# SAGE's neighbour sums over three bf16 pieces of h, and the second attention's scores on VectorE, in a four-layer graph network

## The chip, the cores and the metric

The kernel runs on one core of one Trainium2 chip. The metric is the device time of one execution in microseconds, taken as the median of several runs. The engines are named as in the profile: PE is TensorE (PEld its weight loads), DVE is VectorE, ACT is ScalarE, POOL is GpSimd, and SP issues most of the DMA transfers. L12 is line 12 of the kernel before.

## The reference

The input is x, 3327 nodes of 512 float32 features, and adj, a sparse adjacency matrix. Four layers follow each other, each of the form x = x + layer(relu(layernorm(x)), adj). Layer 0 is a graph attention with 8 heads of 64, followed by a batch normalisation and a relu; layer 1 is SAGE; layers 2 and 3 are graph attentions with an elu. What matters here are SAGE and the scores of layer 2:

```python
# layer 1, x is here h = relu(layernorm(x))
mask = (adj > 0).astype(x.dtype)
deg = jnp.sum(mask, axis=1, keepdims=True)
agg = mask @ x / jnp.maximum(deg, 1.0)
self_f = x @ W_self + b_self
nb_f = agg @ W_nb + b_nb
combined = jnp.concatenate([self_f, nb_f], axis=-1)
out = combined @ W_comb + b_comb
return jax.nn.relu(out)
# layer 2
Wh = jnp.einsum('nd,hdo->hno', x, W)
f1 = jnp.einsum('hno,ho->hn', Wh, a1)
f2 = jnp.einsum('hno,ho->hn', Wh, a2)
e = jax.nn.leaky_relu(f1[:, :, None] + f2[:, None, :], negative_slope=ALPHA)
e = jnp.where(adj[None, :, :] > 0, e, NEG_INF)
attention = jax.nn.softmax(e, axis=-1)
h_prime = jnp.einsum('hnm,hmo->hno', attention, Wh)
```

## The kernel before

Nodes are padded to 3328 and cut into 26 blocks of 128 rows. At the start the kernel builds, from adj, lists of neighbours: each block is two groups of 64 destination rows (GB), and each group has a number of chunks of 128 source rows (CAPS, from 22 for the first group down to 4 for the last; 359 chunks in all). A chunk is fetched by one indirect DMA on GpSimd (`gather`, L1115), which reads 128 rows of a table in DRAM by the indices in a column of `idx`. `mask` (one byte per element, in SBUF) says which of the 128 sources belong to which of the 64 destinations.

The three attentions (`attend`) walk the chunks in batches of three: VectorE makes the weights (L1216, L1223) and TensorE sums the weighted rows (L1237). Their order on TensorE, VectorE and ScalarE is written by hand.

Between the first and second attention lies the region that the change touches. There the order of the instructions on each engine is settled by the framework's scheduler, from the program's order, dependences and buffers. Its steps are these.

- The batch normalisation's variance (`var_ps`, up to about 945 us in the profile).
- `normed(c)` (L1364 and after), for two blocks at a time: VectorE scales and shifts (L1370, L1371), takes the relu and the residual (L1372), the statistics (L1377, L1378), and ScalarE writes h = Relu(r x + ng) (L1385) into `bn_y`. SP stores h to `h_dram` (L1386), 2048 bytes per row, one store of 512 KB per two blocks.
- `own(c)` (L1388 and after), for each block: four transposes (`h_ps`), ScalarE's copy (`hT`, L1393), four 512-column fp32 matmuls with W_self W_comb (`s_ps`, L1396), and VectorE's addition of the bias (L1397). It stands two blocks behind `normed`.
- SAGE's loop. A part is two chunks of each of the block's two groups. `load` takes a row buffer `z_rows` (128 x 2 x 512 float32) and a mask buffer `z_mask` for each group, of which there are SROWS = 8 each, so 16 chunks; ScalarE widens the mask to float32 (L1453), and GpSimd gathers. Loading runs two parts (SAHEAD) ahead. Then, for each chunk in turn of the two groups u = 0 and 1, TensorE does one float32 matmul (L1472), mask 128x64 as weights, rows 128x512 as data, into half the partitions of `sage_acc`: `acc[u * GB : (u + 1) * GB, :]`.
- Ahead of each pair of chunks stands a `tick()`, which advances all that lies beside the loop by one step. The first of it is `ending` (L1409 and after): the mean (`s_ag`, ScalarE), transposes (`a_ps`), copy (`aT`), four matmuls with W_nb W_comb (`n_ps`, L1421), the sum with `own`'s result and the residual on VectorE (L1426, L1427), and the store of x2. The second is the next layer's projection, the class `Following`: `norm` does the layernorm on ScalarE (L777 to L788), and `rest` the remaining six steps: transposes (`p_ps`, L795) and ScalarE's Relu (L798); the scores `p_sd` as four matmuls of 16 columns with WA, a product of W and the attention vectors made at the start (L803), and two exps (L807, L808) and a copy (L810) of them on ScalarE; a clamp (L813) and four matmuls `p_wh` = hW (L816); eight ScalarE multiplications by the exps, one per head, and the store of the table's rows (L820, L821); a transpose `p_tr` (L824); and its copy and store (L827 and after). The PSUM buffers of `Following` are two, shared by `p_ps`, `p_sd`, `p_wh` and `p_tr`.

`following(...)` makes this class, and its constructor loads W (1 MB, `fWt`) by SP. For layer 2 it is called ahead of the variance; for layer 3 the same class runs beside the second attention.

Of the kernel before, what the change touches and what calls it, by code (L numbers as in the profile page):

```python
# [23 lines left out]
F32 = mybir.dt.float32  # L24
BF16 = mybir.dt.bfloat16

F32R = mybir.dt.float32r
I32 = mybir.dt.int32
# [3 lines left out]
AF = mybir.ActivationFunctionType  # L32
ALU = mybir.AluOpType
ET = mybir.EngineType
AX = mybir.AxisListType
# [3 lines left out]
P = 128  # L39
H = 8  # L40
F = 64
D = H * F
# [15 lines left out]
UNIT = 3  # L58
SUNIT = 2
SROWS = 8  # L60
SAHEAD = 2
SMALL = 53.0
SHIFT = 20.0
# [676 lines left out]
class Following:  # L740

    def __init__(self, tc, cs, N, wl, W, WA, table, r_dram, pool, psum, pb=1):
        self.__dict__.update(locals())
        nc = tc.nc
        self.NB = table.shape[0] // P
        self.Wt = pool.tile([P, KC, D], F32, name=f"fWt{wl}")
        nc.sync.dma_start(self.Wt, W.rearrange("(kc p) o -> p kc o", p=P))
        self.hs = pool.tile([P, self.NB, KC], F32, name=f"hs{wl}")  # L750
        self.early, self.ready = [], []
# [4 lines left out]
    def tick(self):  # L756
        for _ in range(min(2, len(self.ready))):
            while self.ready and next(self.ready[0]) is None:
                self.ready.pop(0)
        for g in list(self.early):  # L760
            hx = next(g)
            if hx is not None:
                self.early.remove(g)
                self.ready.append(self.rest(*hx))

    def drain(self):
        while self.early or self.ready:
# [4 lines left out]
    def norm(self, c, xt):  # L772
        nc, pp, cs = self.tc.nc, self.pool, self.cs

        junk = pp.tile([P, D], F32, name="ln_j", tag="ln_j", bufs=1)
        st = pp.tile([P, 4], F32, name="ln_s", tag="ln_s", bufs=3)
        nc.scalar.activation(junk, xt, AF.Identity, accum_out=st[:, 0:1])  # L777
        nc.scalar.mul(st[:, 1:2], st[:, 0:1], -1.0 / D)
        nc.scalar.activation(junk, xt, AF.Square, bias=st[:, 1:2], accum_out=st[:, 2:3])
        step = rsqrt(nc, pp, cs, st[:, 2:3], 1.0 / D)  # L780
        yield
        y = step()
        if c == self.NB - 1:
# [5 lines left out]
        yield c, hx  # L789

    def rest(self, c, hx):
        nc, pp, WA, wl = self.tc.nc, self.pool, self.WA, self.wl
# [294 lines left out]
def sparse(ctx: ExitStack, tc: tile.TileContext, t: dict, out: bass.AP, WA, ls, cs, idx, rdeg, first):  # L1087
# [158 lines left out]
            while ends:  # L1246
                later()

    def following(lx, layer, wl, W, pb=1):
# [5 lines left out]
        return Following(tc, cs, N, wl, W, WA, table, r_dram, pp, pps, pb)  # L1255

    def elu_into(xin, dst, then=lambda c, xt: None):
        def finish(c, hp, pool):
# [17 lines left out]


    wx_dram = dram.tile([2, KC, P, D], F32, name="wx_dram")
    h_dram = dram.tile([NP, D], F32, name="h_dram")
    with ExitStack() as mx:  # L1280
        mid = mx.enter_context(tc.tile_pool(name="fmid", bufs=1))

# [58 lines left out]
        Wx = mid.tile([P, 2, KC, D], F32, name="fWx")  # L1341
        nc.sync.dma_start(Wx, wx_dram.rearrange("k kc p o -> p k kc o"))

        proj = following(mx, 2, 1, t["L2_gnn_W"], 2)
        gp = mx.enter_context(tc.tile_pool(name="fsage", bufs=2))
        gps = mx.enter_context(tc.tile_pool(name="fsage_ps", bufs=2, space=PSUM))
        two = [P, 2, D]
# [15 lines left out]
        with tc.tile_pool(name="fln", bufs=1) as bp:  # L1363


            def normed(c):
                xr = bp.tile(two, F32, name="bn_x", tag="bn_x", bufs=3)
                nc.sync.dma_start(xr, t["x"][c * P : (c + 2) * P, :].rearrange("(k p) o -> p k o", p=P))
                yy = y[:, c : c + 2, :]
                nc.vector.tensor_tensor(yy, yy, gam.unsqueeze(1).to_broadcast(two), ALU.mult)  # L1370
                nc.vector.tensor_tensor(yy, yy, bet.unsqueeze(1).to_broadcast(two), ALU.add)  # L1371
                nc.vector.scalar_tensor_tensor(xr, yy, 0.0, xr, ALU.max, ALU.add)  # L1372
                nc.sync.dma_start(x1[c * P : (c + 2) * P, :].rearrange("(k p) o -> p k o", p=P), xr)
                mv = bp.tile([P, 2, nc.vector.BN_AGGR_DIM], F32, name="ln_mv", tag="ln_mv", bufs=3)
                for i in range(2):
                    st = bp.tile([P, nc.vector.BN_STATS_DIM], F32, name="ln_st", tag="ln_st", bufs=3)
                    nc.vector.bn_stats(st, xr[:, i, :])  # L1377
                    nc.vector.bn_aggr(mv[:, i, :], st)  # L1378
                r = rsqrt(nc, bp, cs, mv[:, :, 1:2].rearrange("p k o -> p (k o)"))()
                if c + 2 == NB:  # L1380
                    nc.vector.tensor_tensor(r[:, 1:2], r[:, 1:2], cs["real"], ALU.mult)
                ng = bp.tile([P, 2, 1], F32, name="ln_ng", tag="ln_ng", bufs=3)
                nc.vector.scalar_tensor_tensor(ng, mv[:, :, 0:1], -1.0, r.unsqueeze(2), ALU.mult, ALU.mult)
                for i in range(2):
                    nc.scalar.activation(yy[:, i, :], xr[:, i, :], AF.Relu, scale=r[:, i : i + 1], bias=ng[:, i, :])  # L1385
                nc.sync.dma_start(h_dram[c * P : (c + 2) * P, :].rearrange("(k p) o -> p k o", p=P), yy)  # L1386

            def own(c):  # L1388
                tp = gps.tile([P, KC, P], F32, name="h_ps", tag="a_ps")
# [14 lines left out]
            for i in range(2):  # L1404
                own(NB - 2 + i)

        ends = []

        def ending(b, acc):  # L1409
# [34 lines left out]
        def load(i):  # L1444
            if i >= len(parts):
                return
            zs = loaded[i] = []
            for u, kn in enumerate(parts[i][1]):
                if kn is not None:
                    k0, n = kn  # L1450
                    zt = gp.tile([P, SUNIT, D], F32, name="z_rows", tag="z_rows", bufs=SROWS)
                    mf = gp.tile([P, SUNIT, GB], F32, name="z_mask", tag="z_mask", bufs=SROWS)
                    nc.scalar.copy(mf[:, :n, :], mask[:, k0 : k0 + n, :])  # L1453
                    for k in range(n):
                        gather(zt[:, k, :], h_dram, k0 + k)
                        zs.append((k, u, k0 + k, mf[:, k, :], zt[:, k, :]))
            zs.sort(key=lambda x: x[:2])
# [3 lines left out]
        for i, (b, _, begins, stops) in enumerate(parts):  # L1461
            load(i + SAHEAD)
            if begins:
                acc = gps.tile([P, D], F32, name="sage_acc", tag="sage_acc")
            at = -1
            for r, u, k, m, z in loaded.pop(i):
                if r != at:
                    at = r
                    tick()
                g = b * PG + u  # L1470
                f, l = k == ls.first[g], k == ls.first[g] + CAPS[g] - 1
                nc.tensor.matmul(acc[u * GB : (u + 1) * GB, :], m, z, start=f, stop=l)  # L1472
            if stops:
                ends.append(ending(b, acc))
        while ends:
# [97 lines left out]
```

## Time and profile before

| | us |
|---|---|
| median of 3 runs (2575.82 to 2585.8) | 2585.0 |
| profiled execution | 2951.92 |
| its span | 2950.1 |
| mean granted TensorE clock in it | 0.791 |

The profiled execution is 367 us longer than the median; all times of instructions below are from it. Its stages, with the busy time of each engine, are:

| stage | us from the start | PE | DVE | ACT | POOL | clock |
|---|---|---|---|---|---|---|
| lists and first projection | 0 to 330 | 213 | 215 | 134 | 25 | 0.79 |
| first attention | 330 to 900 | 413 | 456 | 177 | 334 | 0.81 |
| variance | 900 to 945 | 30 | 24 | 17 | 0 | 0.81 |
| `normed` and most of `own` | 945 to 1025 | 68 | 74 | 35 | 0 | 0.92 |
| rest of `own`, SAGE's loop, second projection | 1025 to 1650 | 518 | 67 | 249 | 339 | 0.92 |
| second attention, third projection | 1650 to 2300 | 480 | 475 | 311 | 340 | 0.76 |
| third attention | 2300 to 2950 | 441 | 471 | 193 | 343 | 0.66 |

A line of the table of stages in the profile gives a window and its length, then for each engine the busy time and the number of instructions, the clock as a share of full speed, the mean busy share of the 16 DMA engines, and GB/s. A line of the groups gives line, engine, operation, out<-in, shapes and count; after the first bar the busy time and the mean ns of one; after the second the idle time of the engine ahead of these instructions and what ended it. A line of the timeline gives start, duration, instruction, and in brackets the idle time before it and what ended it. A line of the DMA queues gives packets, MB, and the time the packets took as a share of 16 engines' time; q0 carries GpSimd's gathers, q1 the transfers of SP.

### The profile page before, as it was taken

The page shows a single profiled execution, that of the slowest core. Times are in us where ns is not written, and L with a number is a line of the kernel's source. Part 1 is how long each engine was busy: PE and PEld are TensorE (multiplying, and loading weights), DVE is VectorE, ACT ScalarE, POOL GpSimd, SP SyncE. Part 2 cuts the span into 40 slices and gives each one's busy share as a digit, 9 for nine tenths or more (in the row PEclk, how much of TensorE's full clock was granted, in tenths as well). Part 3 has the DMA queues.
Part 4 walks back from the last instruction along what each step waited for, and adds up shares of the span by engine and source line. Part 5 has one row for each costly group of instructions (what it writes and reads, how often), then busy time and mean ns, then how long its engine had stood idle before and what let it go on. Part 6 is the DMA issues. An engine that isn't in the chain of part 4 may idle for free.

```text
span 2950.1 us, 54237 instructions
## 1 busy us (share of the span) xinstructions
PE 2161.4 (73%) x21320; PEld 1372.2 (47%) x21320; DVE 1781.5 (60%) x2194; ACT 1115.7 (38%) x4044; POOL 1381.8 (47%) x1482
## 2 busy tenths in 40 slices
PE   4777577767775976888998567877777657767775
PEld 2444354555552422233333355655555345556564
DVE  7648587878786800011111377777776277888886
ACT  4543022333434412344455213555666501232333
POOL 1001365666550055665554365555444066666563
PEclk9778688977777997899999777777787766675765
DMA  7761577877662746666665466666565166667774
GB/s 309 282 251 46 174 235 233 252 214 209 201 203 82 246 145 187 189 207 212 198 196 183 133 184 186 200 198 188 178 178 166 45 192 190 193 200 198 201 205 131
DMA packets 188773, 562.09 MB, mean 191 GB/s; under 512 B 37732, under 2 KB 42272, under 8 KB 185182
## 3 DMA queue, kind: packets, MB, share of 16 engines
q0 software_dynamic: 115456, 404.86, 47.2%
q1 hardware_dynamic: 73054, 153.67, 14.7%
q8 instruction: 171, 2.80, 0.4%
q14 instruction: 92, 0.75, 0.1%
HBM read 498.74 MB, written 59.68 MB: 189 GB/s over the span
## 4 chain that ended last, share of the span: by engine, by line
PE 54%; issue 16%; ACT 9%; another core or an unknown queue 3%; DVE 3%; DMA 2%; POOL 1%; SPq 0%; DVEq 0%; ACTq 0%; POOLq 0%
PE facc L1237 28%; PE p_wh L816 7%; PE sage_acc L1472 5%; PE n_ps L1421 3%; PE r_bc L1148 2%; PE p_sd L803 2%; PE s_ps L1396 2%; ACT v_row L820 2%; ACT fhp L1175 1%; PE fwx_ps L1314 1%; PE bmean_ps L1324 1%; PE p_ps L795 1%; ACT hT L798 1%; DMA rows<-table,idx 1%
## 5 line engine op out<-in xcount | busy, mean ns | idle before, releaser
L1115 POOL DMA_INDIRECT rows<-table,idx x1077 | 1023.4, 950 | 873.2 <-PE facc L1237 361.7
L1237 PE MATMUL facc<-rows,wgt 128*64 128x65 f32 x17232 | 975.3, 268 | 412.7 <-issue 394.5
L1237 PEld LDWEIGHTS facc<-rows,wgt 128*64 128x64 f32 x17232 | 826.5, 176 | 628.7 <-issue 576.9
L1223 DVE TENSOR_TENSOR wgt<-mx,mask 128x1536 f32<-128x1536 f32 (+1 forms) x405 | 638.4, 1576 | 158.6 <-PE facc L1237 75.0
L1216 DVE TENSOR_TENSOR mx<-r_bc,rows 128x1536 f32<-128x1536 f32 (+1 forms) x405 | 639.6, 1579 | 144.7 <-PE facc L1237 65.9
L1115 POOL DMA_INDIRECT z_rows<-h_dram,idx x359 | 339.4, 945 | 387.0 <-ACT hT L1393 139.5
L1175 ACT ACTIVATE fhp<-sums,rd 64x64 f32<-64x64 f32 x832 | 219.8, 334 | 137.0 <-DVE rd L1169 71.8
L1472 PE MATMUL sage_acc<-z_rows,z_mask 128*64 128x512 f32 x718 | 225.2, 639 | 9.5 <-DMA z_rows<-h_dram,idx 6.2
L816 PE MATMUL p_wh<-fWt,hT 128*128 128x512 f32 x416 | 227.7, 695 | 1.4 <-ACT s_col L810 1.4
L1165 ACT COPY sums<-facc 128x260 f32<-128x260 f32 x156 | 57.7, 370 | 405.0 <-PE facc L1237 354.3
L813 DVE TENSOR_SCALAR s_col<-s_col 128x8 f32<-128x8 f32 x52 | 9.2, 177 | 306.0 <-issue 135.9
L1208 ACT ACTIVATE mask<-on 128x192 uint8<-128x192 uint16 (+1 forms) x135 | 46.5, 344 | 378.8 <-DVE on L1202 214.1
L816 PEld LDWEIGHTS p_wh<-fWt,hT 128*128 128x128 f32 x416 | 90.3, 228 | 109.8 <-issue 105.3
L820 ACT ACTIVATE v_row<-p_wh,v_row 128x64 f32<-128x64 f32 x416 | 90.4, 328 | 125.8 <-PE p_wh L816 99.3
L1426 DVE TENSOR_TENSOR s_o<-n_ps,bn_y 128x512 f32<-128x512 f32 x26 | 18.0, 691 | 192.2 <-issue 95.6
L1036 POOL DMA_DIRECT2D list_b<-shift x12 | 5.9, 503 | 273.4 <-DVE shift L990 273.4
L680 PE MATMUL wh_ps<-fWt,hT 128*128 128x512 f32 x208 | 128.9, 777 | 0.0
L803 PE MATMUL p_sd<-WA,hT 128*128 128x16 f32 x416 | 74.4, 303 | 70.3 <-ACT hT L798 46.2
L803 PEld LDWEIGHTS p_sd<-WA,hT 128*128 128x128 f32 x416 | 71.8, 246 | 103.9 <-ACT hT L798 59.6
L1175 ACT ACTIVATE bn_y<-sums,rd 64x64 f32<-64x64 f32 x416 | 109.5, 333 | 2.4 <-DVE rd L1169 0.5
L1421 PE MATMUL n_ps<-fWx,aT 128*128 128x512 f32 x208 | 106.1, 646 | 5.6 <-ACT aT L1417 5.5
L1148 PE MATMUL r_bc<-r_two,fones 2*128 2x512 f32 x156 | 95.3, 615 | 14.8 <-issue 8.1
(198 smaller groups left out, 2108.0 us busy)
## 6 DMA issues: line engine op xcount, KB each, us to landing
adj_i<-in_adj SPq DMA_DIRECT2D x26, 1664.0 KB
table<-v_row SPq DMA_DIRECT2D x78, 264.0 KB
rows<-table,idx POOLq DMA_INDIRECT x1077
fin_x<-fx SPq DMA_DIRECT2D x52, 256.0 KB
ln_x<-in_x SPq DMA_DIRECT2D x26, 256.0 KB
bn_x<-in_x SPq DMA_DIRECT2D x13, 512.0 KB
fx<-bn_x SPq DMA_DIRECT2D x13, 512.0 KB
fsage_x<-fx SPq DMA_DIRECT2D x26, 256.0 KB
```

The lines of the kernel that those rows point to most:

```text
L680: nc.tensor.matmul(wh, hT[:, kc, :], self.Wt[:, kc, :], start=(kc == 0), stop=(kc == KC - 1))
L803: nc.tensor.matmul(sd[:, : 2 * H], hT[:, kc, :], WA[wl][:, kc, :], start=(kc == 0), stop=(kc == KC - 1))
L816: nc.tensor.matmul(wh, hT[:, kc, :], self.Wt[:, kc, :], start=(kc == 0), stop=(kc == KC - 1))
L820: nc.scalar.mul(V[:, h, 0:F], wh[:, h * F : (h + 1) * F], V[:, h, F : F + 1])
L1115: nc.gpsimd.indirect_dma_start(out=dst, out_offset=None, in_=src[:, :], in_offset=bass.IndirectOffsetOnAxis(ap=idx[:, k : k + 1], axis=0))
L1148: nc.tensor.matmul(rb, ones[0:2, :].bitcast(F32R), rrs.pop(g).bitcast(F32R), start=True, stop=True)
L1175: nc.scalar.mul(hp[o0 : o0 + GB, h * F : (h + 1) * F], sm[mine, q, 0:F], rd[mine, q, :])
L1216: nc.vector.tensor_tensor(mx[:, :n], rbs[g].unsqueeze(1).to_broadcast(full), gt[:, :n, H * (F + 1) : ROW].unsqueeze(3).to_broadcast(full), ...
L1223: nc.vector.tensor_tensor(wt[:, :n], mx[:, :n], mk.unsqueeze(2).to_broadcast(full), ALU.mult)
L1237: nc.tensor.matmul(accs[g][v * GB : (v + 1) * GB, q * (F + 1) : (q + 1) * (F + 1)], wt[:, k, h, :], gt[:, k, h * (F + 1) : (h + 1) * (F + 1)],
L1421: nc.tensor.matmul(ps, aT[:, kc, :], Wx[:, 1, kc, :], start=(kc == 0), stop=(kc == KC - 1))
L1472: nc.tensor.matmul(acc[u * GB : (u + 1) * GB, :], m, z, start=f, stop=l)
```

## The change

Each row of h is kept in DRAM as three bf16 pieces, high, middle and low, whose sum is h exactly: the upper halves of the float32 words of h, the upper halves of what remains, and the rest. `h_dram` has rows of 3 x 512 bf16, 3072 bytes. In `normed`, per block, VectorE does two subtractions and ScalarE two copies for that, and there is one store of 384 KB per block. The loop gathers these rows, and each chunk is summed by three bf16 matmuls with a bf16 mask into the same accumulator. For a pair of chunks the order is piece by piece, within a piece group by group.

For layer 2, the second part of `Following` is a new function, `rest_by_rows`. It has no `p_sd`: VectorE multiplies `p_wh` with both attention vectors (broadcast to all partitions, 2 x 256 KB loaded in the constructor), sums over each head's 64 columns, and clamps; and it multiplies by the exps in one instruction in place of ScalarE's eight. It has five steps where `rest` has six. Layer 3 still uses `rest`. `following(...)` for layer 2 is now called behind `normed` and `own`, just ahead of the loop; in the built order of SP's instructions its loads come right behind the last store to `h_dram`.

```diff
@@ Following.__init__
+        if ab is not None:
+            self.ab = pool.tile([P, 2, D], F32, name=f"ab{wl}")
+            for k, a in enumerate(ab):
+                nc.sync.dma_start(self.ab[:, k, :], a.partition_broadcast(P))
@@ Following.tick
-                self.ready.append(self.rest(*hx))
+                self.ready.append((self.rest if self.ab is None else self.rest_by_rows)(*hx))
@@
+    def rest_by_rows(self, c, hx):
...
+        yield True
+        self.mean(c, hT)
+        wh = self.psum.tile([P, D], F32, name="p_wh", tag="p_ps", bufs=self.pb)
+        for kc in range(KC):
+            nc.tensor.matmul(wh, hT[:, kc, :], self.Wt[:, kc, :], start=(kc == 0), stop=(kc == KC - 1))
+        yield True
+        pr = pp.tile([P, 2, D], F32, name="sd_pr", tag="sd_pr", bufs=1)
+        nc.vector.tensor_tensor(pr, wh.unsqueeze(1).to_broadcast([P, 2, D]), self.ab, ALU.mult)
+        sd = pp.tile([P, 2 * H], F32, name="sd_col", tag="sd_col", bufs=2)
+        nc.vector.tensor_reduce(sd, pr.rearrange("p k (h f) -> p (k h) f", f=F), AX.X, ALU.add)
+
+        sf = pp.tile([P, H], F32, name="s_col", tag="s_col", bufs=2)
+        nc.vector.tensor_scalar(sf, sd[:, :H], -SMALL, SMALL, ALU.max, ALU.min)
...
+        rs = halves(nc, pp, self.cs, sf)
+        yield True
+        nc.vector.tensor_tensor(
+            V[:, :, 0:F], wh.rearrange("p (h f) -> p h f", f=F), V[:, :, F : F + 1].to_broadcast([P, H, F]), ALU.mult
+        )
+        nc.sync.dma_start(self.table[c * P : (c + 1) * P, :ROW], row.bitcast(I32))
+        rs = rs()
+        yield True
...
@@ sparse
-    h_dram = dram.tile([NP, D], F32, name="h_dram")
+    h_dram = dram.tile([NP, PIECES * D], BF16, name="h_dram")
@@ ahead of the variance
-        proj = following(mx, 2, 1, t["L2_gnn_W"], 2)
@@ normed
-                nc.sync.dma_start(h_dram[c * P : (c + 2) * P, :].rearrange("(k p) o -> p k o", p=P), yy)
+                for i in range(2):
+                    hi = yy[:, i, :].bitcast(BF16)[:, 1::2]
+                    hp = bp.tile([P, PIECES, D], BF16, name="h_pieces", tag="h_pieces", bufs=2)
+                    rest = bp.tile([P, D], F32, name="h_rest", tag="h_rest", bufs=2)
+                    nc.vector.tensor_tensor(rest, yy[:, i, :], hi, ALU.subtract)
+                    nc.scalar.copy(hp[:, 0, :], hi)
+                    hi = rest.bitcast(BF16)[:, 1::2]
+                    nc.vector.tensor_tensor(hp[:, 2, :], rest, hi, ALU.subtract)
+                    nc.scalar.copy(hp[:, 1, :], hi)
+                    b = c + i
+                    nc.sync.dma_start(h_dram[b * P : (b + 1) * P, :], hp.rearrange("p t o -> p (t o)"))
@@ ahead of SAGE's loop
+        proj = following(mx, 2, 1, t["L2_gnn_W"], 2, (t["L2_gnn_a1"], t["L2_gnn_a2"]))
@@ load
-                    zt = gp.tile([P, SUNIT, D], F32, name="z_rows", tag="z_rows", bufs=SROWS)
-                    mf = gp.tile([P, SUNIT, GB], F32, name="z_mask", tag="z_mask", bufs=SROWS)
+                    zt = gp.tile([P, SUNIT, PIECES * D], BF16, name="z_rows", tag="z_rows", bufs=SROWS)
+                    mf = gp.tile([P, SUNIT, GB], BF16, name="z_mask", tag="z_mask", bufs=SROWS)
@@ SAGE's loop
-            for r, u, k, m, z in loaded.pop(i):
-                if r != at:
-                    at = r
-                    tick()
-                g = b * PG + u
-                f, l = k == ls.first[g], k == ls.first[g] + CAPS[g] - 1
-                nc.tensor.matmul(acc[u * GB : (u + 1) * GB, :], m, z, start=f, stop=l)
+            zs = loaded.pop(i)
+            for r in range(SUNIT):
+                now = [z for z in zs if z[0] == r]
+                if now:
+                    tick()
+                for j in range(PIECES):
+                    for _, u, k, m, z in now:
+                        g = b * PG + u
+                        f = k == ls.first[g] and j == 0
+                        l = k == ls.first[g] + CAPS[g] - 1 and j == PIECES - 1
+                        nc.tensor.matmul(acc[u * GB : (u + 1) * GB, :], m, z[:, j * D : (j + 1) * D], start=f, stop=l)
```

More of the change, by code (lines that the diff above doesn't have):

```diff
@@ L60 @@
 SROWS = 8
+PIECES = 3
 SAHEAD = 2
@@ L740, with __init__ @@
 class Following:
-    def __init__(self, tc, cs, N, wl, W, WA, table, r_dram, pool, psum, pb=1):
+    def __init__(self, tc, cs, N, wl, W, WA, table, r_dram, pool, psum, pb=1, ab=None):
         self.__dict__.update(locals())
         nc = tc.nc
+        if ab is not None:
+            self.ab = pool.tile([P, 2, D], F32, name=f"ab{wl}")
+            for k, a in enumerate(ab):
+                nc.sync.dma_start(self.ab[:, k, :], a.partition_broadcast(P))
         self.NB = table.shape[0] // P
@@ L789, in norm @@
         yield c, hx
+    def rest_by_rows(self, c, hx):
+        nc, pp = self.tc.nc, self.pool
+        tp = self.psum.tile([P, KC, P], F32, name="p_ps", tag="p_ps", bufs=self.pb)
+        for kc in range(KC):
+            nc.tensor.transpose(tp[:, kc, :], hx[:, kc * P : (kc + 1) * P], self.cs["ident"])
+        hT = pp.tile([P, KC, P], F32, name="hT", tag="hT", bufs=2)
+        for kc in range(KC):
+            nc.scalar.activation(hT[:, kc, :], tp[:, kc, :], AF.Relu, accum_out=self.hs[:, c, kc : kc + 1])
+        yield True
+        self.mean(c, hT)
+        wh = self.psum.tile([P, D], F32, name="p_wh", tag="p_ps", bufs=self.pb)
+        for kc in range(KC):
+            nc.tensor.matmul(wh, hT[:, kc, :], self.Wt[:, kc, :], start=(kc == 0), stop=(kc == KC - 1))
[6 more added lines that the diff above has]
+        nc.vector.tensor_scalar(sf, sd[:, :H], -SMALL, SMALL, ALU.max, ALU.min)
+        row = pp.tile([P, ROW], F32, name="v_row", tag="v_row", bufs=2)
+        V = row[:, : H * (F + 1)].rearrange("p (h f) -> p h f", f=F + 1)
+        d = sd[:, H : 2 * H]
+        nc.scalar.activation(V[:, :, F : F + 1], d.rearrange("p (h o) -> p h o", o=1), AF.Exp)
+        nc.scalar.activation(row[:, H * (F + 1) :], d, AF.Exp, scale=-0.8, bias=self.cs["down"])
+        rs = halves(nc, pp, self.cs, sf)
[6 more added lines that the diff above has]
+        yield True
+        tr = self.psum.tile([2 * H, P], F32, name="p_tr", tag="p_ps", bufs=self.pb)
+        nc.tensor.transpose(tr, rs, self.cs["ident"])
+        rr = pp.tile([2 * H, P], F32, name="r_row", tag="r_row", bufs=2)
+        nc.scalar.copy(rr, tr)
+        n = P // GB
+        nc.sync.dma_start(
+            self.r_dram[c * n : (c + 1) * n, :, :, :].rearrange("g t h i -> (t h) g i"),
+            rr.rearrange("h (g i) -> h g i", i=GB),
+        )
+        yield None
@@ L1247, in attend, with following @@
                 later()
-    def following(lx, layer, wl, W, pb=1):
+    def following(lx, layer, wl, W, pb=1, ab=None):
         table = dram.tile([NP, ROW], I32, name=f"table{layer}")
@@ L1254, in following @@
         pps = lx.enter_context(tc.tile_pool(name=f"fproj_ps{layer}", bufs=1, space=PSUM))
-        return Following(tc, cs, N, wl, W, WA, table, r_dram, pp, pps, pb)
+        return Following(tc, cs, N, wl, W, WA, table, r_dram, pp, pps, pb, ab)
     def elu_into(xin, dst, then=lambda c, xt: None):
@@ L1464, in sparse @@
                 acc = gps.tile([P, D], F32, name="sage_acc", tag="sage_acc")
-            at = -1
-            for r, u, k, m, z in loaded.pop(i):
-                if r != at:
-                    at = r
+            zs = loaded.pop(i)
+            for r in range(SUNIT):
+                now = [z for z in zs if z[0] == r]
+                if now:
                     tick()
-                g = b * PG + u
-                f, l = k == ls.first[g], k == ls.first[g] + CAPS[g] - 1
-                nc.tensor.matmul(acc[u * GB : (u + 1) * GB, :], m, z, start=f, stop=l)
+                for j in range(PIECES):
[4 more added lines that the diff above has]
+                        nc.tensor.matmul(acc[u * GB : (u + 1) * GB, :], m, z[:, j * D : (j + 1) * D], start=f, stop=l)
             if stops:
```

## The prediction

> **What bounds the kernel now.** I read first the table of stages (busy time by windows), then the groups of instructions and the waits inside the SAGE loop, then TensorE's and GpSimd's timelines, and last the DMA queues. Columns of the first view: window, length, busy us (and count) of PE, PEld, DVE, ACT, POOL, then the granted TensorE clock, the DMA share and GB/s.
>
> ```profile
> 945.00:1025.00 80.00, 67.97 (x202) 33.71 (x203) 74.09 (x171) 34.67 (x70) 0.40 (x1) 0.92 0.72 252
> 1025.00:1075.00 50.00, 44.92 (x133) 19.96 (x132) 6.92 (x10) 5.42 (x12) 20.38 (x23) 0.97 0.39 116
> 1075.00:1650.00 575.00, 472.73 (x1550) 185.23 (x1547) 59.70 (x184) 243.55 (x1032) 318.65 (x337) 0.91 0.62 191
> ...
> 1092.00:1110.00 18.00, 6.46 (x13) 1.23 (x12) 0.00 (x0) 0.59 (x2) 13.43 (x16) 0.86 0.72 210
> ```
>
> Row one is `normed`: VectorE works 74 of 80 us and bounds it. Row two is the rest of `own` on TensorE, while gathers start. Row three is the loop: TensorE 82% busy at clock 0.91, GpSimd 55%, DMA 62%; no engine fills it alone. The last row is 18 us in which GpSimd issued at full rate: already 0.72 of the DMA engines.
>
> ```profile
> L1472 PE MATMUL sage_acc<-z_rows,z_mask 128*64 128x512 f32 x718 | 225.2, 639 | 9.5 <-DMA z_rows<-h_dram,idx 6.2 <-issue 3.0
> L803 PE MATMUL p_sd<-WA,hT 128*128 128x16 f32 x200 | 29.5, 265 | 12.1 <-issue 12.1
> L820 ACT ACTIVATE v_row<-p_wh,v_row 128x64 f32<-128x64 f32 x192 | 41.6, 326 | 30.5 <-PE sage_acc L1472 19.5 <-remote 7.0 <-PE p_wh L816 4.0
> L1115 POOL DMA_INDIRECT z_rows<-h_dram,idx x353 | 333.8, 946 | 246.0 <-PE sage_acc L1472 92.8 <-issue 83.6 <-PE p_tr L824 46.4
> ```
>
> These groups of the loop show the three things the change replaces, and that GpSimd's idle time ends mostly with TensorE (a row buffer freed by a SAGE matmul). TensorE waits only 6 us for gathered rows: today transfers keep up.
>
> ```profile
> 1253.37 5.37 PE L1472 MATMUL sage_acc<-z_rows,z_mask 128*64 128x512 f32 x24
> ...
> 1287.22 3.68 PE L816 MATMUL p_wh<-fWt,hT 128*128 128x512 f32 x8
> ```
>
> ```profile
> 1024.60 0.94 POOL L1115 DMA_INDIRECT z_rows<-h_dram,idx  x1 [139.47 <-ACT hT L1393]
> 1025.85 0.95 POOL L1115 DMA_INDIRECT z_rows<-h_dram,idx  x1 [0.30 <-issue]
> ```
>
> ```profile
> q0 software_dynamic: 26960, 88.36, 52.1%
> q1 hardware_dynamic: 11545, 19.32, 9.8%
> ```
>
> TensorE: a dense 512-column fp32 record takes 3.68/8 = 0.46 us (0.427 by start times), a SAGE record 5.37/24 = 0.224: the two groups of 64 columns of the array run side by side, so one gather's two records cost 0.43 us. GpSimd: one gather per 0.95 + 0.30 = 1.25 us. DMA (queues within 1075 to 1640): 337 gathers took 52.1% of 565 us, 0.874 us of all 16 engines each for 256 KB; all else took 9.8%, 55 us.
>
> [...] 718 records for 359 matmuls, each record 427 ns[...]. [...] 2048-byte rows [...] cost 0.874 us a gather, table rows of 2112 bytes [...] 0.968 (55.3% of 620 us by 355, in the second attention), rows of 2528 bytes [...] 1.073 (66.7% of 560 by about 348, in the first)[...]. [...] the adds at L1426 measured 691.
>
> **The change, part by part**, in microseconds of the profiled execution.
>
> *Pieces in `normed`.* Added on VectorE: two subtractions of 512 per block, 52 in all. Durations are 0.68 (L1397), but starts of neighbours lie 0.60 apart, so 52 × 0.60 = 31. VectorE bounds this stage, so all of it is on the path. Also on VectorE now: adds of `own` that lay behind 1025 before (six, 3.6), and 5 to 10 of waiting, since the built order has the subtraction behind ScalarE's Relu and copies on both engines. Removed: nothing. ScalarE's 52 copies (estimate 0.6 each from L1393's 0.58, 31) lie beside 34.67 busy of 80: free unless VectorE waits for them. The stores (26 of 384 KB in place of 13 of 512 KB, 3 MB more) end with the stage. So gathers, which need all of h, start at 1024.6 + 42 ≈ 1067. Less than 42 is lost: before, TensorE was busy with `own` until 1073.7 and the 16 row buffers were full, so that only 22 gathers were out by 1075. After, `own` is nearly done by 1067. Net: some 15 gathers, 20 us.
>
> *Where `following` is called.* Its 1 MB of weights, and 0.5 MB for the broadcast vectors, go on SP's queue behind the last h store, onto DMA engines that the first gathers want: 1.5 MB at 300 GB/s (262144/0.874) is 5. Behind them on SP are only the loop's loads and stores, needed some 20 us later: nothing.
>
> *Matmuls.* 359 × 2 records at 0.214 (paired) become 359 × 3 bf16 [...]: per gather 0.43 becomes 0.32; busy time 225 becomes about 169. The trace shows no bf16 matmul in column halves. Upper bound, if they do not pair: 0.65 a gather, more than today; lower: 0.32. I take pairing, since fp32 records pair in the same order. p_sd: −29.5 busy, −26 × 0.86 = 22 by starts.
>
> *ScalarE to VectorE.* ScalarE loses 208 × 0.2 = 41 busy and two copies; VectorE gains per block a 1024 multiply (1.13), a 1024 reduce (1.13) and a 512 multiply (0.60): 26 × 2.9 = 75, beside 60 busy of 575. Hidden; what VectorE does late is the residual add L1426, at worst 2.3 behind a score, and up to that per block (60) if nothing covered it; I take zero, since five ticks of other TensorE work lie between. One step fewer per block shortens the tail at the loop's end by perhaps 2; left out.
>
> *Gathers.* 359 rows-of-128 go from 256 to 384 KB. Issue stays 1.25. Transfer: by bytes [...] 0.874 × 1.5 = 1.31; [...] with a fixed part per row beside the rate of adj's contiguous loads (0 to 120 us: 36.67 MB in 80.3% of the time, 23.8 bytes per ns an engine) 8 × (3072/23.8 + 109 − 86) ns = 1.22. I take 1.31: no row size in the trace is cheaper per byte (0.427, 0.458 and 0.424 ns per byte of row), and this is the same table in the same loop. Other traffic adds 55/359 = 0.15: 1.46. The engines won't be filled wholly; the fullest long stretch (the loads of adj at the start) shows a share of about 0.9, so 1.46/0.90 = 1.62 per gather.
>
> *Sum.* Before, gathers ended with the last s_ag at 1632. After: 1067 + 5 + 1 (first landing) + 359 × 1.62 (582) = 1655. Change +23: span 2950 to 2973, profiled execution 2951.9 to 2975. The median shown, 2585, is 367 below the profiled execution, so I add the difference, not the ratio: 2608. The attentions ran at clock 0.76 to 0.82 in the profile; if the plain runs are granted more, TensorE's relief is worth less there, and bytes cost the same. That speaks for the slower side too.
>
> **Rivals.**
> - *Transfers nearly keep up* (the other side). Price between, 1.40 with the other traffic, at 0.93 filling: 1.505 × 359 = 540, end 1613, −19: 2566. For it: the pace before was 557/337 = 1.65 with 60% of the DMA engines, and ScalarE's and TensorE's steps that freed buffers late get shorter. It decides below a pace of 1.56 per gather.
> - *DMA hardly binds.* [...] For it: TensorE's work per 10-gather block falls from 13.3 to 11.4 by starts, 1.14 per gather, and GpSimd's floor is 1.25. Against: the 0.72 share at full issue, times 1.5, exceeds one.
> - *Pieces don't pair.* TensorE per gather 1.33 + 0.22 − 0.09 = 1.46; at 0.9 filling 1.62 as well: 2608. Slower by another cause.
> - *A wash.* The chain of ScalarE, VectorE and TensorE steps holds the loop, or the pace falls to 1.56 to 1.60: 359 × 1.58 = 567, 2593.
>
> **How the numbers follow.** Chances: transfer-bound 0.43, unpaired 0.06, wash 0.18, nearly keeps up 0.20, hardly binds 0.13. About 0.5% (13 us) is what a measurement can tell from no change. The first two give slower, with a little of the wash: 0.51; the next two faster: 0.33; 0.16 within. The forecast is the first, 2608, its own range 2598 to 2632 (start loss 15 to 35, filling 0.88 to 0.93). The whole range runs from 2540, which leaves out the far part of the hardly-bound case (a still shorter start loss or fuller engines, about 0.06), to 2638, which leaves out transfers priced above linear or a longer start (about 0.12).
>
> **What would show it.** In the profile after: the first gather at 1060 to 1072, VectorE 105 to 115 busy before it; DMA share in the loop at 0.85 or more (before 0.62); q0's time per gather 1.31 [...]; SAGE matmuls waiting for their rows by tens of us in place of 6; GpSimd's waits for sage_acc staying, though TensorE's busy share falls to about 70%; sage records at 0.11 by starts (0.21 means unpaired). It would be wrong if DMA stays below 0.8 while the pace falls under 1.5, or if VectorE's scores make the table's stores late.

## The result, and the profile after

The changed kernel takes 2594.27 us (median of 20 runs, 2579.36 to 2599.34), the kernel before 2575.56 (20 runs, 2572.71 to 2585.8): ratio 1.0056, 95% interval 1.0042 to 1.007. It is slower, by 19 us between the medians and by 14 between the means, to which the ratio is closer. The forecast was slower, 2608.

The execution profiled before the prediction, 2951.92 us, is as long as the kernel before is in the set of experiments e5 to e8, about 2949, while in all other sets here it takes about 2575, so the profile after is compared with a second profile of the kernel before (e1, span 2574.9).

Two lines of each kernel, busy time by windows: the first from the first `normed` instruction to the first gather, the second from the first gather to the last. The kernel before (e1):

```profile
849.34:932.71 83.37, 67.10 (x202) 33.46 (x203) 77.86 (x175) 34.66 (x70) 0.00 (x0) 0.90 0.72 255
932.71:1426.71 494.00, 470.32 (x1581) 183.28 (x1580) 62.30 (x176) 233.56 (x960) 341.15 (x358) 0.99 0.74 228
```

The changed kernel:

```profile
853.33:974.87 121.54, 101.48 (x297) 49.73 (x298) 113.97 (x235) 65.19 (x130) 0.00 (x1) 0.91 0.56 203
974.87:1446.59 471.72, 389.09 (x1660) 156.73 (x1658) 123.74 (x235) 189.24 (x748) 340.81 (x358) 0.92 0.95 339
```

Gathers start 42.2 us later (932.7 to 974.9), VectorE having 114 us to do ahead of them in place of 78. Four of the 42.2 lie ahead of `normed`, whose first instruction came at 849.3 and 853.3; in the other runs of this length it came anywhere between 844.6 and 851.6, with the pieces or without. The loop is 22.3 shorter (494.0 to 471.7). From the last gather to the end it is 1148.2 and 1146.2. So +42.2 − 22.3 − 2.0 = +17.9, the difference of the spans (2592.8 − 2574.9).

Inside the loop, TensorE lost 81 us of work, but its time only 22. Before, it was busy 95% at clock 0.99; now 82% at 0.92, with the DMA engines at 0.95. The groups of the changed loop, and its queues from first gather to last:

```profile
L1166 POOL DMA_INDIRECT z_rows<-h_dram,idx x359 | 341.8, 952 | 310.9 <-ACT hT L1455 180.0 <-issue 69.5 <-PE sage_acc L1538 40.0
L1538 PE MATMUL sage_acc<-z_rows,z_mask 128*64 128x512 bf16 x1077 | 172.2, 410 | 26.4 <-DMA z_rows<-h_dram,idx 26.2
```

```profile
q0 software_dynamic: 28405, 139.68, 83.0%
q1 hardware_dynamic: 11808, 20.03, 11.4%
```

The sums fell from 225.6 (e1) to 172.2 us. A run of 12 bf16 records at clock 1.00 takes 1.49 us (at 1049.59), 0.124 each, where 24 float32 ones took 5.37, 0.224 each (at 1253.37 in the profile before): the bf16 matmuls pair too. A gather of 384 KB took 83.0% × 471.7/358 = 1.094 us of all DMA engines; one of 256 KB in e1 63.7% × 494/358 = 0.879. Where TensorE now stands still is in its waits over 970 to 1530 (total, times, longest):

```profile
PE p_ps L801 <- ACT ln_h L794: 34.3, 12, 4.1
PE sage_acc L1538 <- DMA z_rows<-h_dram,idx: 26.2, 26, 6.7
...
PE p_tr L832 <- DVE r_half L735: 14.2, 7, 3.7
PE a_ps L1478 <- ACT s_ag L1474: 10.7, 11, 2.3
```

Only the second is a wait for gathered rows. The longest such wait, 6.73 us, is at the start of the loop, ahead of the sums at 991.76. While it lasted, from 984 to 992 us, q1, which carries the loads of `following`, took 39.6% of the DMA engines' time, beside the first gathers on q0:

```profile
991.76 3.39 PE L1538 MATMUL sage_acc<-z_rows,z_mask 128*64 128x512 bf16 x12 [6.73 <-DMA z_rows<-h_dram,idx]
```

```profile
q0 software_dynamic: 314, 1.57, 51.1%
q1 hardware_dynamic: 588, 1.14, 39.6%
```

In e1, TensorE's waits from first to last gather are 23.3 us for rows and next to nothing else. One of the new waits, on TensorE's timeline of the changed kernel:

```profile
1091.84 1.98 PE L1484 MATMUL n_ps<-fWx,aT 128*128 128x512 f32 x4
1093.75 1.80 PE L1538 MATMUL sage_acc<-z_rows,z_mask 128*64 128x512 bf16 x13
1099.52 0.44 PE L801 MATMUL p_ps<-fident,ln_h 128*128 128x128 f32 x2 [3.97 <-ACT ln_h L794]
...
1102.54 1.97 PE L809 MATMUL p_wh<-fWt,hT 128*128 128x512 f32 x2
...
1104.77 2.84 PE L809 MATMUL p_wh<-fWt,hT 128*128 128x512 f32 x6
```

and the same place in the kernel before (e1):

```profile
1092.43 1.02 PE L1421 MATMUL n_ps<-fWx,aT 128*128 128x512 f32 x2
1093.38 5.42 PE L1472 MATMUL sage_acc<-z_rows,z_mask 128*64 128x512 f32 x22
1100.28 2.03 PE L1472 MATMUL sage_acc<-z_rows,z_mask 128*64 128x512 f32 x4 [1.47 <-DMA z_rows<-h_dram,idx]
1102.24 0.66 PE L795 MATMUL p_ps<-fident,ln_h 128*128 128x128 f32 x4
```

Between a block's last `n_ps` and the first transpose `p_ps` of its layernorm lies a chain on VectorE and ScalarE (L1489, L1490, L783 to L794) of 5.7 us here: `n_ps` ends at 1093.8, `p_ps` starts at 1099.5. Before, the scheduler put 26 records, 13 gathers' sums, between the two; in the changed kernel 13 bf16 matmuls, 4 gathers. Counted over the built programs: 12 to 14 gathers in each of the first ten blocks before, 4 to 8 after. TensorE waits out the rest, and soon after two `p_wh` records take 1.97 us where six later ones take 2.84. The granted clock shows why. These windows are the wait, the first 0.98 us of work after it, and 3 us each of the slow and of the later `p_wh` records (the clock is the third number from the end):

```profile
1095.55:1099.52 3.97, 0.00 (x0) 0.00 (x1) 0.59 (x3) 3.28 (x11) 3.06 (x4) 1.00 0.82 263
1099.52:1100.50 0.98, 0.98 (x8) 0.45 (x8) 0.00 (x0) 0.00 (x0) 0.68 (x2) 1.00 0.93 341
1101.00:1104.00 3.00, 3.00 (x8) 0.86 (x7) 0.00 (x0) 1.63 (x10) 2.09 (x4) 0.50 1.02 415
1104.50:1107.50 3.00, 3.00 (x8) 1.10 (x7) 0.00 (x0) 0.00 (x0) 2.31 (x3) 1.00 1.01 399
```

After 3.97 us without work TensorE worked 1.3 us at clock 1.00, from 1099.52 to 1100.85; then, in windows of 0.1 us, the clock was half for 3.4 us, from 1100.85 to 1104.26, and 0.98 to 1.00 again behind that. This is what one place shows; what sets when the clock falls, and for how long, isn't shown.

### The profile page after: what moved, and what is told of

It reads as the page before. It is cut to its first block, busy times and chain, and to the rows that moved or that the text cites. A ratio compares the mean times of both kernels' runs of the same rounds, so it can differ in the third digit from the quotient of the medians.

```text
span 2592.8 us, 54553 instructions
## 1 busy us (share of the span) xinstructions
PE 1827.7 (70%) x21471; PEld 1194.8 (46%) x21471; DVE 1883.9 (73%) x2324; ACT 1095.5 (42%) x3862; POOL 1385.4 (53%) x1482
## 4 chain that ended last, share of the span: by engine, by line
PE 27%; DVE 26%; issue 12%; ACT 10%; DMA 7%; POOL 3%; DVEq 0%; SPq 0%; POOLq 0%; ACTq 0%
DVE mx L1267 12%; PE facc L1288 7%; DVE wgt L1274 7%; DMA rows<-table,idx 4%; PE p_wh L867 3%; PE n_ps L1484 3%; PE sage_acc L1538 3%; PE p_wh L809 3%; DMA z_rows<-h_dram,idx 3%; POOL rows L1166 2%; ACT fhp L1226 2%; PE s_ps L1458 1%; PE p_sd L854 1%; ACT v_row L871 1%; ACT bn_y L1226 1%
## 5 line engine op out<-in xcount | busy, mean ns | idle before, releaser
L1288 PE MATMUL facc<-rows,wgt 128*64 128x65 f32 x17232 | 742.9, 257 | 373.2 <-DVE wgt L1274 238.5
L1288 PEld LDWEIGHTS facc<-rows,wgt 128*64 128x64 f32 x17232 | 688.2, 169 | 496.6 <-DVE wgt L1274 289.7
L1538 PE MATMUL sage_acc<-z_rows,z_mask 128*64 128x512 bf16 x1077 | 172.2, 410 | 26.4 <-DMA z_rows<-h_dram,idx 26.2
L1489 DVE TENSOR_TENSOR s_o<-n_ps,bn_y 128x512 f32<-128x512 f32 x26 | 18.0, 692 | 163.0 <-PE n_ps L1484 162.6
L812 DVE TENSOR_TENSOR sd_pr<-p_wh,ab 128x1024 f32<-128x1024 f32 x26 | 31.8, 1225 | 134.5 <-PE p_wh L809 134.5
L1538 PEld LDWEIGHTS <-z_mask 128*64 128x64 bf16 x1077 | 62.7, 113 | 139.2 <-issue 101.8
L1516 ACT CAST z_mask<-mask 128x128 bf16<-128x128 uint8 (+1 forms) x196 | 50.3, 285 | 156.3 <-PE sage_acc L1538 155.3
L867 PE MATMUL p_wh<-fWt,hT 128*128 128x512 f32 x208 | 113.5, 694 | 1.4 <-ACT s_col L861 1.4
L809 PE MATMUL p_wh<-fWt,hT 128*128 128x512 f32 x208 | 108.5, 657 | 1.9 <-DVE hT L700 1.9
L1458 PE MATMUL s_ps<-fWx,hT 128*128 128x512 f32 x208 | 95.8, 615 | 7.3 <-ACT hT L1455 7.3
L1199 PE MATMUL r_bc<-r_two,fones 2*128 2x512 f32 x156 | 86.6, 559 | 7.1 <-DMA r_two<-r_dram 4.0
```

What stands on the lines that cost most here:

```text
L809: nc.tensor.matmul(wh, hT[:, kc, :], self.Wt[:, kc, :], start=(kc == 0), stop=(kc == KC - 1))
L867: nc.tensor.matmul(wh, hT[:, kc, :], self.Wt[:, kc, :], start=(kc == 0), stop=(kc == KC - 1))
L1199: nc.tensor.matmul(rb, ones[0:2, :].bitcast(F32R), rrs.pop(g).bitcast(F32R), start=True, stop=True)
L1288: nc.tensor.matmul(accs[g][v * GB : (v + 1) * GB, q * (F + 1) : (q + 1) * (F + 1)], wt[:, k, h, :], gt[:, k, h * (F + 1) : (h + 1) * (F + 1)],
L1458: nc.tensor.matmul(ps, hT[:, kc, :], Wx[:, 0, kc, :], start=(kc == 0), stop=(kc == KC - 1))
L1538: nc.tensor.matmul(acc[u * GB : (u + 1) * GB, :], m, z[:, j * D : (j + 1) * D], start=f, stop=l)
```

## Experiments

Five sets of runs, each set timed beside the kernel before; the table has four of them. Gathers are given as start of the first, then the time from first to last, in us; "the loop" below is this time. The expectations speak of four theories: A, the pieces delay the start and the loop itself is quicker; B, the bytes fill the DMA engines and hold the loop; C, TensorE still holds it; D, formed after e11, the built order leaves the layernorm chain uncovered.

| run | ratio (95% interval) | first gather | first to last |
|---|---|---|---|
| e1 kernel before | | 932.7 | 494.0 |
| e9 changed kernel again | 1.0052 (1.0035 to 1.0069) | 971.6 | 480.6 |
| e2 pieces only | 1.0176 (1.0158 to 1.0193) | 968.4 | 499.8 |
| e3 new scores only | 0.9923 (0.9909 to 0.9937) | 931.9 | 473.0 |
| e4 two pieces moved | 0.9981 (0.9972 to 0.999) | 964.5 | 454.6 |
| e10 no subtractions | 1.0015 (1.0005 to 1.0026) | 943.7 | 484.0 |
| e11 two of three summed | 1.0134 (1.0114 to 1.0154) | 965.9 | 495.8 |
| e12 scores, 11 buffers | 0.9899 (0.9882 to 0.9916) | 933.1 | 459.0 |
| e13 changed, written order | 1.0246 (1.0221 to 1.0271) | 972.1 | 504.8 |
| e14 same, two moved | 1.0232 (1.0211 to 1.0253) | 968.7 | 510.6 |
| e15 same, GpSimd's pieces | 1.0297 (1.028 to 1.0315) | 968.2 | 524.3 |
| e16 written order, longer chain | 1.0155 (1.0133 to 1.0178) | 964.5 | 480.0 |
| e17 same, two moved | 1.0151 (1.013 to 1.0172) | 969.5 | 482.3 |
| e18 scores in that order | 1.0011 (1.0001 to 1.0021) | 931.2 | 476.6 |

In the set at 2949 us: e5 (as e10) 1.0045 (1.0028 to 1.0061), e6 (as e11) 0.9974 (0.995 to 0.9998), e7 0.9932 (0.9915 to 0.995), e8 (as e12) 0.9879 (0.9859 to 0.99).

### The two halves apart: e1, e2, e3

e1 is the kernel before, unchanged.

> The kernel before again, unchanged, for a profile at the clock of the plain runs. Both theories need it: time 2575 to 2586. Theory A (the pieces in normed delay the gathers, the loop itself is quicker): the first gather about 35 to 45 us earlier than in the changed kernel (974.9), near 935, and the gathers last longer than the changed kernel's 473 us, near 490 to 500. Theory B (the bytes fill the DMA engines and slow the loop): the first gather near 950, and the gathers last less than 473 us.

Measured: first gather 932.7, 494.0 us to the last. Theory A's figures, both. e2 takes the new scores out:

```diff
-        proj = following(mx, 2, 1, t["L2_gnn_W"], 2, (t["L2_gnn_a1"], t["L2_gnn_a2"]))
+        proj = following(mx, 2, 1, t["L2_gnn_W"], 2)
```

> The pieces without the new scores: layer 2 uses the old rest (p_sd on TensorE, eight multiplications on ScalarE). Theory A: the scores on VectorE help the loop a little, so this is slower than the changed kernel by up to 10 us: ratio to before 1.006 to 1.011. Theory B: the loop runs at the DMA engines' pace, the scores don't matter: 1.005 to 1.007.

Both missed: 1.0176. With the old scores the loop, 53 us of sums lighter, is not shorter at all:

```profile
968.41:1468.16 499.75, 428.39 (x1835) 184.76 (x1834) 56.61 (x168) 229.95 (x953) 342.29 (x358) 0.88 0.91 320
```

TensorE is busy 86% where it was 95%, at clock 0.88 where it was 0.99, and waits 39 us for `ln_h`. e3 is the kernel before with `rest_by_rows`, and `following` called ahead of the loop; h stays in float32.

```diff
-        proj = following(mx, 2, 1, t["L2_gnn_W"], 2)
...
+        proj = following(mx, 2, 1, t["L2_gnn_W"], 2, (t["L2_gnn_a1"], t["L2_gnn_a2"]))
```

> The new scores alone, h in float32 rows of 2048 bytes, following called ahead of the loop. Theory A (TensorE's p_sd and ScalarE's multiplications held the loop): faster than before by 10 to 25 us, ratio 0.990 to 0.996. Theory B, in which the loop before is held by the SAGE matmuls and the gathers: within 5 us, 0.998 to 1.002.

0.9923, as Theory A had it. The loop takes 473.0 us, as long as the changed kernel's:

```profile
931.94:1404.89 472.95, 436.41 (x1396) 159.59 (x1396) 126.37 (x240) 192.68 (x752) 340.23 (x358) 0.97 0.78 241
```

So the scores are worth 20 us, and by the ratios the pieces cost 1.3% beside the new scores and 1.8% beside the old, 33 to 45 us. They bring nothing to the loop beside either kind, and delay it: from `normed`'s first instruction to the first gather it is 83.4 us in e1 and e3, but 119.8 in e2, 119.9 in e9 and 121.5 in the first profile of the changed kernel, so 36 to 38 more.

### Which part of the scores: e7

```diff
-        for h in range(H):
-            nc.scalar.mul(V[:, h, 0:F], wh[:, h * F : (h + 1) * F], V[:, h, F : F + 1])
+        if wl == 1:
+            nc.vector.tensor_tensor(
+                V[:, :, 0:F], wh.rearrange("p (h f) -> p h f", f=F), V[:, :, F : F + 1].to_broadcast([P, H, F]), ALU.mult
+            )
...
```

> The kernel before with following called ahead of the loop and, in layer 2's projection only, ScalarE's eight multiplications as one of VectorE; p_sd stays on TensorE. If TensorE holds the loop before (470 of 494 us busy), only p_sd's 22 to 29 us were worth something: ratio to before 0.998 to 1.001. If ScalarE's steps held it: 0.991 to 0.995, as with the whole of the new scores.

0.9932, in the set at 2949 us, with `p_sd` still on TensorE. That is the range for ScalarE's multiplications holding the loop there, but it isn't shown: the loop of its profile, 576.6 us, is only 9 shorter than the 586.0 of the first profile, where the time fell by 22 (2949.16 to 2926.93), and the call of `following` moved too. Where the kernel before takes 2575 us and TensorE is 95% busy in the loop, this edit wasn't tried.

### The start: e5 and e10

```diff
-                    nc.vector.tensor_tensor(rest, yy[:, i, :], hi, ALU.subtract)
                     nc.scalar.copy(hp[:, 0, :], hi)
-                    hi = rest.bitcast(BF16)[:, 1::2]
-                    nc.vector.tensor_tensor(hp[:, 2, :], rest, hi, ALU.subtract)
                     nc.scalar.copy(hp[:, 1, :], hi)
...
+                    nc.sync.dma_start(h_dram[b * P : (b + 1) * P, 2 * D :], hp[:, 1, :])
```

> The changed kernel without its two subtractions per block on VectorE: the middle and the low piece are copies of the high one, so the sums are of other numbers. ScalarE's copies, all bytes and all matmuls stay; SP issues one store more per block. Theory A (VectorE's 52 subtractions are what delays the gathers): the first gather at 938 to 945 in place of 974.9, the loop as long as before it (about 472), ratio to before 0.990 to 0.996. Rival (ScalarE's copies, or the stores of 3072-byte rows, delay it): the first gather stays later than 955, ratio above 1.000.

e5 is of the set at 2949 us, and has no changed kernel beside it. But e6 below is of the same set and has the changed kernel's `normed`: from its first instruction to the first gather it is 98.1 us in e5 and 120.6 in e6. e10 is e5's edit in a set at 2575.

> As the run without the two subtractions before, now beside the changed kernel on one chip. Theory A (they delay the gathers): first gather 30 to 37 us earlier than in the changed kernel, and that many us off its time if the loop runs at the same pace. Rival (the loop's pace takes it back, since it starts with more of the sums of own still to do on TensorE): first gather as early, but less than 15 us off the time.

The first gather comes 28 us earlier than in e9 and 31 earlier than in the first profile, but 5 to 7 of these lie ahead of `normed`. From its first instruction e10 takes 97.4 us, against 119.9 and 121.5: the subtractions are 22 to 24 of the 36 to 38. The other 14 (97.4 against 83.4 in e1) go with what e10 keeps, the copies and the stores, of which it has one more per block; these weren't taken apart. The ratio missed Theory A's range. Of the time, 13 us come back (2591.0 to 2577.59), fewer than the rival's 15; in the profiled executions 25 (2597.6 to 2572.5). That the loop takes part of it back isn't settled: the changed kernel's own loop varies between 471.7 and 480.6.

### Bytes, matmuls or order: e4, e6, e11, e13 to e17

e4 stores and gathers two of the three pieces, and sums the low one twice.

```diff
-    h_dram = dram.tile([NP, PIECES * D], BF16, name="h_dram")
+    h_dram = dram.tile([NP, 2 * D], BF16, name="h_dram")
...
-                        nc.tensor.matmul(acc[u * GB : (u + 1) * GB, :], m, z[:, j * D : (j + 1) * D], start=f, stop=l)
+                        nc.tensor.matmul(acc[u * GB : (u + 1) * GB, :], m, z[:, min(j, 1) * D : (min(j, 1) + 1) * D], start=f, stop=l)
```

> Leaves the high piece out of what is stored and gathered (rows of 2 pieces, 2048 bytes) and sums the low piece twice, so that VectorE, ScalarE and TensorE do the same work with two thirds of the bytes. Theory A (the start is what costs): the loop is held by GpSimd at 1.25 us a gather and by TensorE; gain over the changed kernel 10 to 20 us, ratio 0.998 to 1.002. Theory B (bytes hold the loop): gain 25 us or more, ratio below 0.996, DMA share in the loop about 0.7.

0.9981: by the ratios a gain of 19 us over the changed kernel, which is at the edge of Theory A's range and short of Theory B's. But the loop, 454.6, near GpSimd's 359 × 1.25 = 449, is 17 us shorter than with all the bytes, so they stayed in question. And the built order is another too: with smaller gathers the scheduler again puts 11 to 15 gathers between `n_ps` and `p_ps` in the first blocks, and TensorE waits 75 us for rows and never for `ln_h`. e11 (and e6) leave the third matmul out and keep the bytes.

```diff
-                for j in range(PIECES):
+                for j in range(PIECES - 1):
```

> The changed kernel with only two of the three matmuls per gathered chunk; the low piece is stored and gathered but not summed. Theory B (bytes hold the loop): gathers still take 465 to 472 us from first to last, ratio to before 1.003 to 1.007, TensorE's clock below 0.92. Theory C (TensorE still holds it): TensorE loses 359 x 0.12 = 43 us, the gathers take 450 to 455 (GpSimd's floor 449), ratio 0.997 to 1.000.

> As the run with two of the three matmuls before, now beside the changed kernel on one chip. Theory B (bytes hold the loop): within 5 us of the changed kernel. Theory C (TensorE holds it): 15 to 25 us less than the changed kernel.

e6 came out at 0.9974 where the kernel before takes 2949 us, with no changed kernel beside it. In e11 neither theory's figure came: less work made the kernel 19 us slower than e9. Its waits and e9's:

```profile
PE p_ps L801 <- ACT ln_h L794: 56.5, 14, 4.5
```

```profile
PE p_ps L801 <- ACT ln_h L794: 34.1, 11, 4.1
```

The matmuls that went had covered the chain; the clock fell from 0.90 to 0.85. This overturned both theories, and gave Theory D, that the order left the chain uncovered. To test bytes in one order, e13 and e14 take the loop's order as written, on TensorE, VectorE and ScalarE:

```diff
+        with tc.manual_schedule(engines={ET.PE, ET.DVE, ET.Activation}):
             for i in range(SAHEAD):
                 load(i)
...
```

> The changed kernel with SAGE's loop in the program's own order on TensorE, VectorE and ScalarE in place of the scheduler's. Theory D (with larger gathers the scheduler put only the matmuls of 4 to 6 gathers between a block's last n_ps and the first transpose of its layernorm, where the kernel before has 12, and TensorE stands still for that chain and falls in clock): now 8 gathers stand there in every block, the waits of p_ps for ln_h fall from 34 us to below 15, the gathers take 450 to 462 us in place of 472 to 481, ratio to before 0.995 to 1.001. Theory B (the bytes hold the loop): the gathers still take 468 us or more, ratio 1.003 to 1.008, TensorE waits for rows in place of ln_h.

> The same written order with two thirds of the bytes: the high piece is neither stored nor gathered and the low one is summed twice, so the sums are of other numbers and the engines' work is that of the run above. Only the bytes differ, not the order. Theory D: within 6 us of the run above. Theory B: 15 to 25 us less than it, the gathers near GpSimd's floor of 449.

Both loops got longer. With 8 gathers in between, `p_ps` still waits 33 and 25 us for `ln_h`, where less than 15 was expected, and `a_ps` and `p_tr` wait 25 and 20 us from first gather to last, in place of 10 and 6. The bytes made no difference: 504.8 and 510.6, with DMA at 0.91 and 0.72. e16 and e17 lengthen the chain by four ticks, so that 11 or 12 gathers cover it in every block:

```diff
             nc.scalar.mul(ag, acc, rdeg[:, b : b + 1])
             yield
+            yield
...
+        if self.ab is not None:
+            yield
+            yield
         yield c, hx
```

(and one more ahead of `p_tr`).

> The changed kernel in the written order, with four ticks more in a block's chain (one ahead of a_ps, two ahead of p_ps, one ahead of p_tr), so that 12 gathers' matmuls cover the layernorm chain in every block, as in the kernel before. Theory D (uncovered chains hold the changed loop): TensorE's waits for ln_h, s_ag and r_half nearly vanish, the gathers take 450 to 462 us, ratio to before 0.995 to 1.001. Theory B (the bytes hold it): 468 us or more, with TensorE's waits for rows above 60 us and DMA above 0.93; ratio 1.003 to 1.008.

> The same order with two thirds of the bytes (the high piece left out, the low one summed twice, so the sums are of other numbers). Theory D: within 6 us of the run above. Theory B: 12 to 25 us less than it.

The waits for `ln_h` are gone. Of the other steps' waits some are left, against the expectation: in both runs 22 to 23 us for `aT`, 13 to 14 for `s_ag`, 4 for `r_half`. e16's window, then e17's:

```profile
964.52:1444.47 479.95, 377.08 (x1644) 157.73 (x1642) 120.84 (x229) 185.18 (x732) 341.67 (x359) 0.91 0.93 333
```

```profile
969.46:1451.75 482.29, 384.94 (x1645) 161.14 (x1644) 121.48 (x229) 186.10 (x733) 341.24 (x359) 0.89 0.75 235
```

DMA at 0.93 or 0.75, TensorE's waits for rows 59 or 55 us, and the same time (medians 2613.9 and 2613.2). In two orders, then, with loops of 480 to 511 us, the added bytes do not set the pace; a DMA share of 0.93 was no bound there. Theory D is only half borne out: covering the chain took 25 us off e13's loop, but not to 450 to 462, and TensorE waits for rows instead, in both. GpSimd is the near floor: 449 of 480 us. Of the other 31 in e16, about 16 are waits for row buffers that sums free and 12 waits that end with `p_tr`, each less the 0.30 that follows every gather.

### Versions to gain by: e8, e12, e15, e18

e8 and e12 are e3 with 11 row buffers loaded three parts ahead.

```diff
-SROWS = 8
-SAHEAD = 2
+SROWS = 11
+SAHEAD = 3
```

> The new scores alone (h in float32) with 11 row buffers in place of 8 and loading three parts ahead in place of two. If TensorE holds this loop (436 of 473 us busy, waiting 32 for rows) and the waits for rows come from too few buffers, the gathers take 450 to 460 us, ratio to before 0.985 to 0.990; if the waits are those of a chain of steps, it stays within 0.2% of the scores alone (0.9923).

> As the run with the new scores alone and 11 row buffers before, now beside the changed kernel: 0.985 to 0.990 of the kernel before, so 1.5 to 2% less than the changed kernel. With the gathers' 1.25 us a chunk as the floor, 450 to 465 us from the first gather to the last where the kernel before takes 494.

0.9879 at 2949 us and 0.9899 at 2575: faster than both kernels. The loop takes 459.0 us, TensorE busy at clock 0.99:

```profile
933.13:1392.08 458.95, 425.28 (x1380) 155.14 (x1379) 123.96 (x235) 190.76 (x742) 341.30 (x359) 0.99 0.79 247
```

Its interval overlaps e3's, so the buffers' own part (14 us of loop) isn't sure in the time; behind the last gather e12 takes 8.5 us longer than e3 (1158.3 and 1149.8). e15 lets GpSimd do the subtractions (e13 with `nc.gpsimd` for `nc.vector` in both).

> The changed kernel in the written order, and with the two subtractions per block on GpSimd, which is idle there, in place of VectorE. If GpSimd takes less than 1.5 us for each of 52, the first gather comes at 938 to 955 in place of 972 to 975, and the ratio is 0.985 to 0.993, about the best seen; if GpSimd is slower than 2 us each or slows VectorE, the first gather comes at 960 or later and the ratio is above 0.995.

GpSimd took 1.42 and 1.44 us in the mean for the two subtractions, but the first gather came at 968.2, 120 us after `normed`'s first instruction and no earlier. VectorE beside it got slower (L1421 at 1.66 us in the mean, against 1.22 in the changed kernel), and though the 34 us of subtractions were gone from it, it waited 31.2 us for `s_ps` between 840 and 1000, against 12.1 in the changed kernel; what holds the start there isn't settled. e18 is e12 in e16's order.

> The new scores alone (h in float32, one row of 2048 bytes), 11 row buffers, in the same written order with the longer chains. TensorE's float32 sums hold this loop (425 of 459 us busy in the scheduler's order): the same as with the scheduler's order, 0.988 to 0.993; above 0.995 if the written order costs by itself.

1.0011: the written order with its longer chain costs 1.1% by itself, 18 us of it in the loop (476.6), so the written orders tell of bytes, not of how fast the loop could be.

## Why the prediction was off

- *Bound of the loop before: right for the trace, wrong for the plain runs.* The trace I worked from gave 586 us for 359 gathers (1.64 each, clock 0.92), with no engine filling the loop; in e1 it is 494 (1.38, clock 0.99), and TensorE is 95% busy.
- *Pieces in `normed`: near.* 42 was forecast, and that the first gather came 42.2 later is partly luck: from `normed`'s first instruction it is 36 to 38. The subtractions are 22 to 24 of it (e10), where 31 was worked out; the rest, 14, is in the range of the 9 to 14 put on other work and waits.
- *`following`'s place: seen where rows land, not where gathers are issued.* The first 16 gathers follow each other at 1.25 us, and the next waits are 0.69 and 1.01. But its loads fall on these gathers, and TensorE waited 6.73 us for rows (7.03 in e9) where they ran, a quarter of the loop's 26.2. In e3, which has the same loads, 2048-byte rows and more of `own` still to do, all 31.5 us of its waits for rows come after 965, 33 us behind the first gather. What this wait cost the loop isn't shown.
- *Matmuls: right.* They pair: 225 to 172 us busy, 169 forecast. That a bf16 record takes half the time of a float32 one was my estimate; measured are 0.124 and 0.224 us. What was missing is that the time doesn't follow (e2).
- *ScalarE to VectorE: hidden, as forecast*, and a gain, which I gave no size of its own: 20 us (e3).
- *Gathers: the step that failed.* "I take 1.31" became 1.094, below even 1.22, the estimate from a fixed part per row; "won't be filled wholly", 0.90, became 0.95; so 1.62 per gather became 471.7/358 = 1.32. Its sign, TensorE waiting for rows by tens of us more, didn't come: 26.2 us, against 23.3 in e1. And the mechanism fell where it could be tried: at equal order, bytes didn't count (e13 with e14, e16 with e17). In its place the traces show GpSimd's issue, 449 us, and buffers freed late beside a layernorm chain that the built order, with larger gathers, left uncovered. That this order is the cause of the 472 to 481 us is argued from e4, e11 and the waits; the changed kernel in the old order of the scheduler wasn't tried. Nor is it shown that the bytes would leave a quicker loop alone: the changed kernel's transfers took 94.7% × 471.7 = 447 us of all DMA engines, an estimate of their floor that is as high as GpSimd's.
- *The sum came near by cancelling.* After, 582 us were forecast, 110 too many; before, 607 had been counted from first gather to last s_ag. Their difference was −25, measured −22. So +23 stood against +19 measured, and 2594 lies just below the 2598 to 2632 given for this case. The rest of the 14 us between 2608 and 2594 is the median that I added to: 2585.0 from 3 runs, 2575.56 from 20.
- *Rivals.* "Hardly binds" agrees with the pairs of equal order in that DMA isn't the limit (0.93 and 0.75 of the DMA engines, 480 and 482 us, in e16 and e17), and was wrong in expecting a gain; the trace before didn't show the price of a gather that it took. The wash named a chain of ScalarE, VectorE and TensorE steps, and gave 2593, but by a pace of 1.58 where 1.32 was measured; I put it at 0.18, because I looked at what TensorE would no longer do, and not at what stood between `n_ps` and `p_ps` in the built order.

## What to carry to other kernels

Work taken from the bound engine may have been the cover of a chain on other engines: count, in the built order, what stands between the producer and the consumer of that chain before and after, since a scheduler may reorder it all when one transfer grows, as this one did. A high DMA share is not shown to be a bound until a run with fewer bytes in the same order is faster; at 0.93 and at 0.75 the loop here took the same time (e16, e17). And a change that pays in a loop but puts work on the engine that bounds the stage ahead of it must be costed there first; here splitting the two halves showed one worth keeping.

## What was not expected of the hardware

- The price of a gather of 128 rows grew by 1.24 for 1.5 times the bytes: 0.879 us for 2048-byte rows (e1), 1.094 for 3072 (changed kernel).
- TensorE's granted clock was lower where it waited more: 0.97 to 0.99 in the loops with 24 to 49 us of waits (e1, e3, e12, e18), 0.85 to 0.93 in the other loops at 2575, with 71 to 115. With less to do, matmuls took longer: an `n_ps` record 685 ns in the mean in e11, 605 in e1 (980 to 1400).
- A GpSimd subtraction of 128 x 512 took 1.42 to 1.44 us in the mean, single ones 1.03 to 2.08, and VectorE's 1024-wide multiplication beside it 1.66 in the mean, in place of 1.22 (e15, changed kernel).
